# Moving state updates, one product and the weight sums between stages of a fused decoder layer

## The chip, the cores and the metric

The kernel runs on one core of a Trainium2 chip. A core has five engines that run side by side, each with its own queue of instructions: TensorE (PE in the profile, with PEld for its weight loads), VectorE (DVE), ScalarE (ACT), GpSimd (POOL) and SyncE (SP), which here issues nearly all DMA transfers. The metric is the device time of one execution in microseconds (us).

## The reference, cut to what matters

The layer works on x of shape (16, 256, 512), that is 4096 tokens of width 512, in fp32. It has three parts, each followed by a layer norm. The first is the one that the change touches, a state-space block:

```
xn   = x * rsqrt(mean(x*x) + EPS) * w_norm
proj = xn @ W_in.T                       # z (1024), xi (1024), dt (16), B (256), C (256)
xi   = silu(causal_conv4(xi))
dt   = softplus(dt + dt_bias);  dA = exp(dt * -exp(A_log))
u    = (dt * mean_over_head(xi))[..., None] * B
h_t  = dA_t * h_(t-1) + u_t ;  y_t = sum_n(h_t * C_t)      # a scan over 256 tokens
y    = (y @ W_h2i.T) * silu(z)
out  = y @ W_out.T + x
```

The second part is a long convolution with gating and the third a linear layer with a routed low-rank update; the change leaves both as they are.

## The kernel before, in words

**Groups.** The state-space block is worked in eight groups `g` of 512 tokens (two sequences of 256), in the loop of line 495. The second and third parts follow as 32 steps, from line 1062.

**Stages.** The large input product is split over ten pairs of output blocks. One pass over the list `order` (lines 561 and 562) is ten stages `i` = 0 to 9: x0, z0, x1, x2, z1, x3, then b0 (stage 6), c1 (stage 7), z2 (8), z3 (9). Each pair is multiplied by a Strassen-like scheme with seven half-size products in place of eight. The first four products (`first_products`) fill two PSUM banks `al` and `be`; `first_sums` reads those (one ScalarE copy, three VectorE adds, lines 319 to 322); `last_products` then adds the other three products on top, and `last_sums` reads these (one ScalarE operation, two VectorE adds, lines 332 to 334). So TensorE can't start the last products of a pair until VectorE has done that pair's first sums.

**Shift between the engines.** In stage `i` TensorE does the first products of pair `i` and then the last products of pair `i-1`. VectorE does the first sums of pair `i` and then the last sums of pair `i-1`; after an x pair it also does the convolution of two channel blocks (`mixed`, one scaling and six multiply-adds for the two, lines 524 to 528, partly on ScalarE).

**States.** In stages 6 and 8 `head_means` forms the head means on TensorE (line 538) for the two halves `ht` of the state rows. In stage 7 `states(0, ...)` and in stage 8 `states(1, ...)` run on VectorE. Each is `m = xm * dtS` (line 549), `B = B * m` (line 550) and two scans over 256 tokens (line 553). `outputs(ht)` multiplies the states by C (line 558). C is the output of pair 7, whose last sums VectorE does in stage 8 (`finish_sums`, line 618). In stage 9 TensorE sums the products over the state index into `yps` (line 596, two instructions for each half), in its queue behind the first products of pair 9 and in front of the last products of pair 8.

**Decays.** The generator `decays` (line 380) makes dt and dA on VectorE and ScalarE in small steps, writes them to DRAM (line 418) and issues three spreading loads (`spread`, line 430) into a pool of three buffers. The fourth, `spread(1, 1)`, is dA for the second half and reuses the buffer of the first, so SyncE holds it until `m` of the first half has been computed. For groups 1 to 7 these steps run in the output product of the previous group; in group 0 they run in stages 1, 2, 3, 5 and 6.

**Weight sums.** The Strassen scheme needs sums of weights. GpSimd forms those of the input weights (`weight_sums`, lines 213 to 216; those of z2 and z3 stand in the program in stages 6 and 7 of group 0), and of the output weights (`w_o_sums`, lines 270 to 278, in stage 8 of group 0). The output product of the group (`out_begin`, `out_middle`, line 685) uses `(0, 1)`, which holds the sum T3 in place, first, and then T1, T2 and T4.

**Order.** The order of the work on each engine is that of the program; no scheduler reorders it. Each engine takes its queue in order, and semaphores tie the engines.

Of the kernel before, what the change touches and what calls it, by code (L numbers as in the profile page):

```python
# [10 lines left out]
ALU = mybir.AluOpType  # L11
# [4 lines left out]
B, S, D = 16, 256, 512  # L16
# [49 lines left out]
def decoder_kernel(  # L66
# [24 lines left out]
    nc = tc.nc  # L91
# [73 lines left out]
    with ExitStack() as s1:  # L165
# [36 lines left out]
        A11, A12, A22, S3, S1, S2, S4 = range(7)  # L202
# [47 lines left out]
        HC = NI // 2  # L250
# [13 lines left out]
        parts = [q2.tile([P, 2, S], F32, tag="vT", name="w_o_sum") for _ in range(2)]  # L264
        parts += [q3.tile([P, 3, S], F32, tag="cT", name="w_o_sum") for _ in range(3)]
        parts = [t[:, k, :] for t in parts for k in range(t.shape[1])]
        for k, name in enumerate(("T1", "T2", "T4")):
            w_o[name] = parts[k * HC : (k + 1) * HC]

        def w_o_sums():  # L270

            sub = nc.gpsimd.tensor_tensor
            for c in range(HC):
                sub(w_o["T1"][c], w_o[0, 1][c], w_o[0, 0][c], ALU.subtract)
                sub(w_o[0, 1][c], w_o[1, 1][c], w_o[0, 1][c], ALU.subtract)
            for c in range(HC):
                sub(w_o["T2"][c], w_o[1, 1][c], w_o["T1"][c], ALU.subtract)
                sub(w_o["T4"][c], w_o[1, 0][c], w_o["T2"][c], ALU.subtract)
        xis = [p1.tile([P, GB, S + 3], F32, name=f"xi{i}") for i in range(4)]
        for t in xis:  # L280
            nc.gpsimd.memset(t[:, :, 0:3], 0.0)
# [35 lines left out]
        def first_sums(al, be, to):  # L317
            u = p2.tile([P, S], F32, tag="u", name="u", bufs=3)
            nc.scalar.copy(u, al[:, 0:S])
            nc.vector.tensor_tensor(u, u, al[:, S:], ALU.add)  # L320
            nc.vector.tensor_tensor(to[3], u, be[:, S:], ALU.add)
            nc.vector.tensor_tensor(to[3], to[3], be[:, 0:S], ALU.add)
            return u
# [56 lines left out]
        def decays():  # L380

            d_lg = ps_t.tile([P, 2, P], F32, tag="tr", name="d_lg")
            d, lg = d_lg[:, 0, :], d_lg[:, 1, :]
            for kc in range(KD):
                for q in range(TT):
                    nc.tensor.matmul(
                        d[32 * q : 32 * (q + 1), :],
                        w_dt[:, kc, :],  # L390
                        xnT[:, kc, q * P : (q + 1) * P],
                        start=(kc == 0),
                        stop=(kc == KD - 1),
                    )
            yield
            two = p1.tile([P, 2, P], F32, tag="two", name="two")
            e, u1 = [p1.tile([P, P], F32, tag=n, name=n) for n in ("e", "u1")]
            dt, dA = two[:, 0, :], two[:, 1, :]
            nc.vector.tensor_scalar_add(dt, d, dtb)
            nc.vector.scalar_tensor_tensor(e, dt, -1.0, dt, ALU.mult, ALU.max)  # L400
            nc.scalar.activation(e, e, AF.Exp, scale=-1.0)
            yield
            nc.vector.tensor_scalar_add(u1, e, 1.0)
            nc.scalar.activation(lg, u1, AF.Ln)
            yield
            same = dA
            nc.vector.tensor_scalar(same, u1, 1.0, None, ALU.is_equal)
            nc.vector.tensor_tensor(lg, lg, same, ALU.add)
            nc.vector.scalar_tensor_tensor(u1, u1, -1.0, same, ALU.add, ALU.add)
            nc.vector.reciprocal(u1, u1)  # L410
            nc.vector.tensor_tensor(lg, lg, u1, ALU.mult)
            nc.vector.tensor_tensor(lg, lg, e, ALU.mult)
            nc.vector.scalar_tensor_tensor(dt, dt, 0.0, lg, ALU.max, ALU.add)
            yield

            nc.scalar.activation(dA, dt, AF.Exp, scale=A)
            for q in range(TT):
                nc.sync.dma_start(
                    both[:, :, q * P : (q + 1) * P].rearrange("x h t -> h x t"),
                    two[32 * q : 32 * q + H1],  # L420
                )
            spreads[:] = [spread(*a) for a in ((0, 0), (1, 0), (0, 1))]
            yield
# [3 lines left out]
        def spread(x, ht):  # L427

            t = p2.tile([P, GT], F32, tag="spread", name="spread", bufs=3)
            nc.sync.dma_start(  # L430
                t,
                both[x, ht * HH : (ht + 1) * HH, :].unsqueeze(1).to_broadcast([HH, NST, GT]),
            )
            return t
# [60 lines left out]
        for g in range(NG):  # L495
# [48 lines left out]
                    )  # L544
                return xm

            def states(ht, xm, dtS, dAS):
                m = p2.tile([P, GT], F32, tag="acc", name="m", bufs=6)
                nc.vector.tensor_tensor(m, xm, dtS, ALU.mult)
                nc.vector.tensor_tensor(Bs[ht], Bs[ht], m, ALU.mult)  # L550
                for b in range(GB):
                    one = Bs[ht][:, b * S : (b + 1) * S]
                    nc.vector.tensor_tensor_scan(
                        one, dAS[:, b * S : (b + 1) * S], one, 0.0, ALU.mult, ALU.add
                    )
# [26 lines left out]
            for i, (kind, p) in enumerate(order):  # L582
# [21 lines left out]
                    finish_products()  # L604
                to = places(kind, p)
                u = first_sums(al, be, to)
                if g == 0:
                    if i == 1:
                        parts = decays()
                    if i in (1, 2, 3, 6):  # L610
                        next(parts)
                    if i == 6:
                        weight_sums(nc.gpsimd, w_z, 2)
# [7 lines left out]
                if g == 0 and i == 7:  # L621
                    weight_sums(nc.gpsimd, w_z, 3)
                if i == 7:
                    states(0, ms[0], *spreads[:2])
                    spreads.append(spread(1, 1))
                if i == 8:
                    outputs(0)
                    states(1, ms[1], *spreads[2:])
                    outputs(1)
                    if more:  # L630
                        rt = to_dram(rms(xs_next))
                    if g == 0:
                        w_o_sums()
                before = (kind, p, al, be, u, to)
                if i < 2 and late:
                    normalised(g - 1, late.pop(0))
# [46 lines left out]
            def out_product(ps, n, a, b, start=False, stop=False, upon=False):  # L683
                for c in range(HC):
                    nc.tensor.matmul(  # L685
                        ps,
                        own[a][c][:, n * P : (n + 1) * P],
                        w_o[b][c],
                        start=start and c == 0,
                        stop=stop and c == HC - 1,  # L690
                        skip_group_check=upon,
                    )

            def out_begin(n):

                al, be = [
                    bank() if n else ps_s.tile([P, 512], F32, tag="s", name="s")
                    for _ in range(2)
                ]
                out_product(al[:, 0:S], n, (0, 0), (0, 0), start=True)  # L700
                out_product(be[:, S:], n, "S3", (0, 1), start=True)
                return al, be

            def out_middle(n, al, be):
# [578 lines left out]
```

## Time and profile before

The time before is 1504.72 us, the median of three runs (1504.67 to 1504.87). The page describes one profiled execution.

| what | value |
|---|---|
| median of the runs | 1504.72 us |
| the profiled execution's own time | 1506.76 us |
| its span, first to last instruction | 1505.0 us |
| mean granted TensorE clock | 0.998 |
| TensorE busy | 1484.1 us, 99% |
| TensorE weight loads busy | 936.7 us, 62% |
| VectorE busy | 1184.4 us, 79% |
| ScalarE busy | 372.1 us, 25% |
| GpSimd busy | 363.3 us, 24% |
| HBM traffic over the span | 64 GB/s |

The page gives the busy time of each engine, the span in forty slices, the chain of work that ended last, and groups of instructions by line. The list of waits says, for each engine and line, how long the engine sat idle and which instruction ended that, with the total, the number of times and the longest, all in us. The timeline gives start and duration in us, engine, line, what is written and read, the shape, and how often the instruction is repeated; idle time before it stands in brackets. The first part takes the span up to about 770 us, one group being about 93 us.

### The profile page before, as it was taken

Reading aid. Unit: us, or ns where it says so; the run is one execution under the profiler, and the core shown is the slowest. Engines: PE = TensorE matmul, PEld = TensorE weight load, DVE = VectorE, ACT = ScalarE, POOL = GpSimd, SP = SyncE. Lnnn points to the kernel's source line nnn. Section 1 sums busy time; section 2 is a strip of 40 time slices with the busy share of each in tenths; the row PEclk is TensorE's granted clock in tenths of the full one; section 3 lists DMA queues with packets and bytes.
Section 4 is the critical chain, followed back from the end, with each engine's and each line's share of the span. In section 5 each row is a group of like instructions: output and inputs, shape, how many; then the busy total and the mean of one; then the engine's idle time right before and its main releaser. Section 6 shows DMA issues by size and latency. Waiting matters only on the chain.

```text
span 1505.0 us, 18707 instructions
## 1 busy us (share of the span) xinstructions
PE 1484.1 (99%) x6952; PEld 936.7 (62%) x6952; DVE 1184.4 (79%) x2132; ACT 372.1 (25%) x843; POOL 363.3 (24%) x528
## 2 busy tenths in 40 slices
PE   9999999999999999999999999999999999999997
PEld 8778788787887878878754444444444444444443
DVE  5978778787787877878667787788788778778776
ACT  2523223232232322323101122122122122122121
POOL 7140010100101001010012343343343243243242
PEclk9999999999999999999999999999999999999999
DMA  8014111121111211112022212212212212212200
GB/s 284 30 36 132 23 64 43 36 79 31 56 42 36 79 43 51 36 36 86 8 95 70 80 54 77 82 53 77 84 49 78 84 50 77 84 50 78 84 32 21
DMA packets 50810, 97.46 MB, mean 65 GB/s; under 512 B 10656, under 2 KB 15008, under 8 KB 50720
## 3 DMA queue, kind: packets, MB, share of 16 engines
q1 hardware_dynamic: 50192, 96.28, 20.1%
q8 instruction: 54, 0.88, 0.2%
q14 instruction: 36, 0.29, 0.1%
q10 hardware_dynamic: 528, 0.00, 0.0%
HBM read 78.95 MB, written 17.32 MB: 64 GB/s over the span
## 4 chain that ended last, share of the span: by engine, by line
PE 89%; DVE 3%; POOL 3%; issue 3%; DMA 1%; SPq 0%; POOLq 0%; ACT 0%; DVEq 0%; ACTq 0%
PE y L899 22%; PE mm L297 16%; PE y L913 12%; PE s L297 9%; PE base L1103 7%; PE s L685 6%; PE mm L685 5%; PE base L1059 2%; PE gl L1098 2%; PE tr L983 1%; PE mm L771 1%; PE mm L644 1%; PE xm L538 1%; PE tr L140 1%; DMA w_f<-in_WffnT 1%
## 5 line engine op out<-in xcount | busy, mean ns | idle before, releaser
L899 PE MATMUL y<-kv 128*128 128x512 f32 x768 | 348.4, 597 | 0.3 <-DVE pr L946 0.3
L946 DVE TENSOR_TENSOR pr<-y,cT 128x1024 f32<-128x1024 f32 x126 | 148.5, 1220 | 131.3 <-PE y L913 126.0
L899 PEld LDWEIGHTS y<-kv 128*128 128x128 f32 x768 | 141.4, 191 | 159.5 <-issue 155.4
L913 PE MATMUL y<-kv 64*64 64x512 f32 x1536 | 181.3, 602 | 3.1 <-DVE pr L946 1.6
L152 DVE TENSOR_TENSOR kv<-vT,cT 128x1024 f32<-128x1024 f32 x128 | 150.4, 1217 | 1.5 <-ACT vT L142 1.5
L528 DVE SCALAR_TENSOR_TENSOR acc<-xi,wc,acc 128x512 f32<-128x512 f32 x192 | 145.2, 770 | 5.7
L956 DVE TENSOR_REDUCE red<-pr 128x128 f32<-128x1024 f32 x126 | 147.1, 1209 | 0.0
L913 PEld LDWEIGHTS y<-kv 64*64 64x64 f32 x1536 | 52.5, 132 | 122.9 <-issue 97.0
L1103 PE MATMUL base<-w_f,ol 128*128 128x512 f32 x248 | 111.5, 592 | 0.0
L297 PE MATMUL mm<-XT,w_z 128*128 128x256 f32 x384 | 90.7, 379 | 0.0
L345 POOL TENSOR_TENSOR rstd<-ms,nhalf 128x4 f32<-128x4 f32 x8 | 8.1, 1018 | 294.5 <-DVE ms L343 294.5
L297 PEld LDWEIGHTS mm<-XT,w_z 128*128 128x128 f32 x384 | 73.0, 190 | 9.9
L61 POOL TENSOR_TENSOR rs_a<-ve_a,nhalf 128x1 f32<-128x1 f32 x32 | 19.0, 593 | 244.8 <-DVE ve_a L59 244.8
L827 POOL TENSOR_TENSOR sk<-kv,skip_bc 128x512 f32<-128x512 f32 x32 | 47.4, 1480 | 116.9 <-DVE kv L152 116.9
L1103 PEld LDWEIGHTS base<-w_f,ol 128*128 128x128 f32 x248 | 44.8, 190 | 44.5 <-issue 44.5
L297 PE MATMUL mm<-xnT,w_z 128*128 128x256 f32 x288 | 70.2, 380 | 1.2 <-DVE u L320 1.2
L969 POOL TENSOR_SCALAR nm_c<-sum_c 128x1 f32<-128x1 f32 x31 | 7.2, 232 | 249.4 <-DVE x L1023 249.4
L297 PEld LDWEIGHTS mm<-xnT,w_z 128*128 128x128 f32 x288 | 54.6, 190 | 12.6 <-issue 3.8
L297 PE MATMUL s<-XT,w_xi 128*128 128x256 f32 x256 | 60.5, 379 | 0.4 <-DVE XT L206 0.4
L297 PE MATMUL mm<-XT,w_xi 128*128 128x256 f32 x256 | 60.5, 379 | 0.0
L974 ACT ACTIVATE sq<-x,nm_c 128x512 f32<-128x512 f32 x31 | 22.4, 722 | 136.8 <-POOL nm_c L969 132.5
L297 PEld LDWEIGHTS s<-XT,w_xi 128*128 128x128 f32 x256 | 48.6, 190 | 7.3 <-POOL w_xi L216 0.8
(258 smaller groups left out, 2544.7 us busy)
## 6 DMA issues: line engine op xcount, KB each, us to landing
kv<-in_toep SPq DMA_DIRECT2D x32, 640.0 KB
cT<-in_ctxT SPq DMA_DIRECT2D x32, 384.0 KB
xt<-in_x SPq DMA_DIRECT2D x32, 256.0 KB
xnT<-in_xT SPq DMA_DIRECT2D x8, 1024.0 KB
spread<-both SPq DMA_DIRECT2D x32, 256.0 KB
first<-xt SPq DMA_DIRECT2D x32, 256.0 KB
vn<-first SPq DMA_DIRECT2D x32, 256.0 KB
out<-res SPq DMA_DIRECT2D x31, 256.0 KB
```

Source lines behind the costliest of these rows:

```text
L152: last = nc.vector.tensor_tensor(kv[:, q, k * BQ : (k + NL // 2) * BQ], vT[:, q, blks].rearrange("p k (b i) -> p (k b) i", i=NH).unsqueeze ...
L297: nc.tensor.matmul(ps, w[:, p, a, kc, :], Xs[b][:, kc, :], start=start and kc == 0, stop=stop and kc == 1, skip_group_check=upon,)
L528: nc.vector.scalar_tensor_tensor(acc, xi[:, :, k : k + S], wc[:, c, k : k + 1], acc, ALU.mult, ALU.add)
L685: nc.tensor.matmul(ps, own[a][c][:, n * P : (n + 1) * P], w_o[b][c], start=start and c == 0, stop=stop and c == HC - 1, skip_group_check=upon,
L827: nc.gpsimd.tensor_tensor(sk, own, skip_bc[:, h * NH : (h + 1) * NH].unsqueeze(1).to_broadcast(full), ALU.mult,)
L899: nc.tensor.matmul(bank_of(y, lb), T[:, PAIRS.index((lb, mb)), :], moving(kv, q, mb), start=not late and lb not in begun, stop=stop, skip_ ...
L913: return nc.tensor.matmul(bank_of(y, lb)[cols], T[rows, len(PAIRS) + lb, cols], moving(kv, q, lb)[rows], start=start, stop=False, skip_gro ...
L946: nc.vector.tensor_tensor(pr.rearrange("p (k b j) i -> p k b j i", k=2, j=NH), y[i].rearrange("p k (b j i) -> p k b j i", j=NH, i=NH), cT[ ...
L956: nc.vector.tensor_reduce(red[:, q, 2 * i : 2 * i + 2, :].rearrange("p k t -> p (k t)"), pr, AX.X, ALU.add)
L1059: nc.tensor.matmul(base, turned[0], w_lb, start=False, stop=True)
L1098: nc.tensor.matmul(gl, o_l[:, kc, :], w_gl[:, kc, :], start=(kc == 0), stop=(kc == KD - 1))
L1103: nc.tensor.matmul(base, o_l[:, kc, :], w_f[:, kc, :], start=(kc == 0), stop=False)
```

## The change

There are four edits. (1) The first multiplication of `states` becomes a function of its own, `stepped`. For the first half it moves from stage 7 to stage 6 in groups 1 to 7 (in front of the last sums of pair 5), and in group 0 to a place further ahead in stage 7 (in front of the last sums of pair 6); the load `spread(1, 1)` moves with it. (2) In stage 8 the whole of `states(1, ...)` moves from behind `outputs(0)` to a place in front of the last sums of pair 7. (3) In `decays` one product moves from VectorE to GpSimd, `e = u1 * e`, and the product ahead of it is written to SBUF instead of PSUM. (4) The sum T3 of the output weights gets its own tiles and is made first, ahead of the other work of GpSimd in stage 8; T1 takes the place of the weights that it is made from. The number of instructions on the large engines stays the same, apart from the one product that changes engine.

```diff
--- before.py
+++ after.py
@@ -264,18 +264,23 @@
         parts = [q2.tile([P, 2, S], F32, tag="vT", name="w_o_sum") for _ in range(2)]
         parts += [q3.tile([P, 3, S], F32, tag="cT", name="w_o_sum") for _ in range(3)]
         parts = [t[:, k, :] for t in parts for k in range(t.shape[1])]
-        for k, name in enumerate(("T1", "T2", "T4")):
+        for k, name in enumerate(("T3", "T2", "T4")):
             w_o[name] = parts[k * HC : (k + 1) * HC]
 
         def w_o_sums():
 
             sub = nc.gpsimd.tensor_tensor
+            w_o["T1"] = w_o[0, 1]
+            for c in range(HC):
+                sub(w_o["T3"][c], w_o[1, 1][c], w_o[0, 1][c], ALU.subtract)
+            yield
             for c in range(HC):
                 sub(w_o["T1"][c], w_o[0, 1][c], w_o[0, 0][c], ALU.subtract)
-                sub(w_o[0, 1][c], w_o[1, 1][c], w_o[0, 1][c], ALU.subtract)
             for c in range(HC):
                 sub(w_o["T2"][c], w_o[1, 1][c], w_o["T1"][c], ALU.subtract)
                 sub(w_o["T4"][c], w_o[1, 0][c], w_o["T2"][c], ALU.subtract)
+            yield
+
         xis = [p1.tile([P, GB, S + 3], F32, name=f"xi{i}") for i in range(4)]
         for t in xis:
             nc.gpsimd.memset(t[:, :, 0:3], 0.0)
@@ -408,9 +413,9 @@
             nc.vector.tensor_tensor(lg, lg, same, ALU.add)
             nc.vector.scalar_tensor_tensor(u1, u1, -1.0, same, ALU.add, ALU.add)
             nc.vector.reciprocal(u1, u1)
-            nc.vector.tensor_tensor(lg, lg, u1, ALU.mult)
-            nc.vector.tensor_tensor(lg, lg, e, ALU.mult)
-            nc.vector.scalar_tensor_tensor(dt, dt, 0.0, lg, ALU.max, ALU.add)
+            nc.vector.tensor_tensor(u1, lg, u1, ALU.mult)
+            nc.gpsimd.tensor_tensor(e, u1, e, ALU.mult)
+            nc.vector.scalar_tensor_tensor(dt, dt, 0.0, e, ALU.max, ALU.add)
             yield
 
             nc.scalar.activation(dA, dt, AF.Exp, scale=A)
@@ -544,9 +549,12 @@
                     )
                 return xm
 
-            def states(ht, xm, dtS, dAS):
+            def stepped(xm, dtS):
                 m = p2.tile([P, GT], F32, tag="acc", name="m", bufs=6)
                 nc.vector.tensor_tensor(m, xm, dtS, ALU.mult)
+                return m
+
+            def states(ht, m, dAS):
                 nc.vector.tensor_tensor(Bs[ht], Bs[ht], m, ALU.mult)
                 for b in range(GB):
                     one = Bs[ht][:, b * S : (b + 1) * S]
@@ -604,6 +612,14 @@
                     finish_products()
                 to = places(kind, p)
                 u = first_sums(al, be, to)
+                if i == 8:
+                    states(1, stepped(ms[1], spreads[2]), spreads[3])
+                if i == 6 and g:
+                    ms = [stepped(ms[0], spreads[0])]
+                    spreads.append(spread(1, 1))
+                if i == 7 and not g:
+                    ms = [stepped(ms[0], spreads[0])]
+                    spreads.append(spread(1, 1))
                 if g == 0:
                     if i == 1:
                         parts = decays()
@@ -621,16 +637,17 @@
                 if g == 0 and i == 7:
                     weight_sums(nc.gpsimd, w_z, 3)
                 if i == 7:
-                    states(0, ms[0], *spreads[:2])
-                    spreads.append(spread(1, 1))
+                    states(0, ms[0], spreads[1])
+                if g == 0 and i == 8:
+                    w_sums = w_o_sums()
+                    next(w_sums)
                 if i == 8:
                     outputs(0)
-                    states(1, ms[1], *spreads[2:])
                     outputs(1)
                     if more:
                         rt = to_dram(rms(xs_next))
                     if g == 0:
-                        w_o_sums()
+                        next(w_sums)
                 before = (kind, p, al, be, u, to)
                 if i < 2 and late:
                     normalised(g - 1, late.pop(0))
@@ -698,7 +715,7 @@
                     for _ in range(2)
                 ]
                 out_product(al[:, 0:S], n, (0, 0), (0, 0), start=True)
-                out_product(be[:, S:], n, "S3", (0, 1), start=True)
+                out_product(be[:, S:], n, "S3", "T3", start=True)
                 return al, be
 
             def out_middle(n, al, be):
```

## The prediction

> **What bounds the kernel.** The page first: one engine fills the span.
>
> ```profile
> PE 1484.1 (99%) x6952; PEld 936.7 (62%) x6952; DVE 1184.4 (79%) x2132; ACT 372.1 (25%) x843; POOL 363.3 (24%) x528
> ```
>
> The chain that ended last gives PE 89%. Only time in which PE stands still, 1505.0 - 1484.1 = 20.9 us, can be won here, since no edit removes a matmul. The list of waits of PE says where; of its twelve lines these three touch the edits:
>
> ```profile
> PE yps L596 <- DVE b L558: 4.5, 8, 1.0
> PE mm L297 <- DVE u L320: 1.2, 1, 1.2
> PE s L685 <- POOL w_o_sum L277: 0.9, 1, 0.9
> ```
>
> The first comes once a group, 1.0 in group 0 and 0.5 in the others. The timeline of group 2 from the end of stage 8, VectorE alone:
>
> ```profile
> 260.12 1.27 DVE L553 TENSOR_TENSOR_SCAN b<-spread,b 128x256 f32<-128x256 f32 x2
> 261.31 0.39 DVE L320 TENSOR_TENSOR u<-u,mm 128x256 f32<-128x256 f32 x1
> ...
> 264.25 0.42 DVE L333 TENSOR_TENSOR c<-u,mm 128x256 f32<-128x256 f32 x1 [1.56 <-PE mm L297]
> 264.58 0.41 DVE L334 TENSOR_TENSOR c<-u,mm 128x256 f32<-128x256 f32 x1
> 264.92 0.69 DVE L558 TENSOR_TENSOR b<-b,c 128x512 f32<-128x512 f32 x1
> 265.52 0.69 DVE L549 TENSOR_TENSOR m<-xm,spread 128x512 f32<-128x512 f32 x1
> 266.24 0.69 DVE L550 TENSOR_TENSOR b<-b,m 128x512 f32<-128x512 f32 x1
> 266.96 1.27 DVE L553 TENSOR_TENSOR_SCAN b<-spread,b 128x256 f32<-128x256 f32 x2
> 268.27 0.69 DVE L558 TENSOR_TENSOR b<-b,c 128x512 f32<-128x512 f32 x1
> ```
>
> and PE of the same stretch:
>
> ```profile
> 267.50 1.02 PE L596 MATMUL yps<-b,sel 128*128 128x512 f32 x2
> 269.02 1.13 PE L596 MATMUL yps<-b,sel 128*128 128x512 f32 x2 [0.50 <-DVE b L558]
> 269.98 0.59 PE L297 MATMUL mm<-xnT,w_z 128*128 128x256 f32 x2
> ```
>
> VectorE idles 1.56 us for C, then does the second half's states, which need no C; PE waits for their end. In group 0 VectorE is a stage behind and has no such hole. The timeline there, same six multiply-adds three times:
>
> ```profile
> 41.30 6.08 DVE L528 SCALAR_TENSOR_TENSOR acc<-xi,wc,acc 128x512 f32<-128x512 f32 x6
> 49.78 4.57 DVE L528 SCALAR_TENSOR_TENSOR acc<-xi,wc,acc 128x512 f32<-128x512 f32 x6
> 61.36 4.56 DVE L528 SCALAR_TENSOR_TENSOR acc<-xi,wc,acc 128x512 f32<-128x512 f32 x6
> ```
>
> The first has GpSimd's sums of z2 and z3 beside it (38.1 to 45.25), the others nothing.
>
> **What the Trainium skill says.** "SBUF — State Buffer", section "SBUF: two separate sides": VectorE with two SBUF inputs and GpSimd exclude each other for a whole instruction. The trace agrees: with GpSimd busy throughout (24.97) the six take 6.77, and a GpSimd sum 1.17 in place of 0.73; VectorE's sums with a PSUM input keep 0.42. "TensorE: Matmul & The Clock Gate", section "Architectural detail": VectorE and GpSimd are strict FIFO; so a waiting GpSimd product holds everything behind it. "GPSIMD Engine Reference", section "4.1 Engine selection": GpSimd can't touch PSUM, hence `u1` as its input.
>
> **Part 1, groups 1 to 7.** Removed: the first `m` (0.68) leaves stage 7. In stage 6 it falls between 249.25 (end of L322) and 250.97, where VectorE waits 1.72 us for PE: free, its inputs being long there (xm ended at 244.7, its load is of the previous group). Without that cover it would cost 0.7 of VectorE, against 4.3 us by which PE's next user (last products of pair 7 at 261.35, L320 done at 257.04) is later. Stage 7 ends 0.7 earlier; L320 of stage 8 can start at 260.7, L322 ends at about 261.95. Then `m` 0.72, `b` 0.72, scans 1.3 (steps from start to start): 264.7. PE has C's products ready at 264.2, so the C sums run without a wait: 0.67, outputs 0.60 + 0.70, done at 266.7 against 268.96. The `spread(1, 1)` moves past no other issue on SP (none stands between stages 1 and 8) and goes out at about 250; before it went at 259.31 and its traffic ended at 262.4, so it is never late.
>
> PE reaches `yps` at 267.50 and now needs no stop. Eight matmuls of 512 columns elsewhere (139.91 to 143.34) step by 0.429; four end at 267.50 + 1.715 = 269.215, and the next now starts at 269.98. Gain 0.765, more than the listed 0.50, because ends of matmuls are modelled and the first step after a stop is 0.1 longer. Seven groups: **-5.4 us**. What is late next? SP's row load moves up with VectorE; the next input load, the output product and the 32 steps hang on PE and shift with it. I find no second wait behind this one. Bounds: 7 x 0.50 = -3.5 to 7 x 0.80 = -5.6; I take -5.4.
>
> **Part 2, GpSimd product, groups 1 to 7.** No row shows it. GpSimd's 128x512 difference takes 1.27 and its 128x256 0.73, so 128x128 about 0.46; with signals of 0.08 and 0.04 (112.12 to 112.20, 227.01 to 227.04), VectorE's next starts 0.58 after L411 instead of 0.36: +0.22. Bounds: 0 to +0.7 (a GpSimd operation on 4 columns takes 1.02). Behind it on VectorE stand the norm statistics and the next first sums (L320 done at 214.45, PE needs it at 216.76): 2.3 us of cover, 0 us paid. Only in group 1 does PE stop on that chain (131.05, 0.3 us after the even step): **+0.2**.
>
> **Part 3, group 0.** The product stands in stage 5, ahead of z2's and z3's sums in GpSimd's queue. These ran at 38.1; now they wait for L411, about 56.4. So:
> - The multiply-adds at 41.30 and the scaling ahead of them run alone: from 40.35 to the next L320 5.00 instead of 6.94, -1.94. PE's stop at 47.76 (even step 46.36; with a slow start 1.6 lost) goes.
> - The multiply-adds of stage 6 start at 60.84 - 1.94 + 0.22 = 59.1. GpSimd has z2's sums until 60.3 (PE needs them at 62.9), z3's with 1.16 each until 65, then T3's. So 7.23 (24.43 to 31.66) instead of 5.00: end at 66.35, 0.5 later than 65.84.
> - PE's second head means (67.39) need the silu of that result, 0.8 later: 67.15. PE waits there from 65.8. Of the 1.6 won, 0.25 is left.
> - From here VectorE runs without a hole as before, 10.67 to the end of outputs(1): 77.0 instead of 76.5. Both halves of `yps` now wait: the second starts at 77.25 instead of 76.57: **+0.7**. The fourth spread load lands about 3 us after issue (its traffic ran from 69.8 to 71.4 after an issue near 68.5); the scan needs it at 73.8.
> - T3 is done by 68.5. But I don't believe that the 0.9 at 88.02 is T3's: L275 ended at 83.70, while VectorE's L334, which reads the `be` bank to be overwritten, ended at 87.93, delayed by sums at 83.77 that took 3.49 for 1.43 beside GpSimd. T1, T2 and T4 still run there, to 87.5: **-0.15**. If it is T3's, -1.1.
>
> **Sum.** -5.4 + 0.2 + 0.7 - 0.15 = -4.65 us. The profiled span of 1505.0 becomes 1500.35; what lies around it (1506.76 - 1505.0 = 1.76) stays, and this execution is 2.04 above the median. The difference carried to the median: 1504.72 - 4.65 = **1500.1**.
>
> **Rivals.**
> - Group 0 gains too. If the exclusion in stage 6 costs less than 7.23 (sums and multiply-adds interleave), up to -1.6 at 47.76, -1.3 at `yps` and -1.1 at 88.02 are kept: 1496.5 to 1499.0. For it: the list books two of these on work that moves. Against: at 24.97 full exclusion was measured. 15%.
> - The gain is half. The wait at `yps` is worth its listed 0.50, or group 0 loses 2 to 3 through the head means: 1501.5 to 1504.0. For it: group 0 has no hole for anything added. 17%.
> - Slower: GpSimd's product holds VectorE in each group. Place: between L411 and L413. It decides when it costs over 2.3 us a group, the cover of PE's last products of pair 0; above that each 0.43 costs 7 x 0.43 = 3.0, and part 1's gain must be spent first (0.77), so from about 3.5 us: 1508. Against: the dearest GpSimd operation of such size took 1.4. 4%.
> - The edits do nothing: the program order does not set VectorE's order, or PE's wait comes from elsewhere; 1504.7. Against: VectorE's timeline follows the program everywhere. 4%.
>
> **How the numbers follow.** The main case, 1499.0 to 1501.5, has 60%. No change means within 0.2%, 3.0 us, about what a measurement of this kernel can tell. Main case and the first rival are faster, and a fifth of the second: 0.78. The rest of it and the last: 0.17; slower 0.05. The range 1498.2 to 1502.6 leaves out the far end of the first rival, half of the second and the last two.
>
> **What would show it.** Right: no `yps` wait in groups 1 to 7, VectorE's hole before the C sums gone, `m` of the first half in the hole of stage 6; in group 0 z2's sums after 56, no stop at 47.76, a new stop at the second head means, a longer one at `yps`. Wrong: a `yps` wait left in later groups, PE idle in stages 7 or 8, or group 0 ending more than 2 us later than before.

## The result, and the profile after

The changed kernel takes 1501.61 us, the median of 13 runs (1500.02 to 1504.75), against 1504.82 us of the kernel before in the same comparison (13 runs, 1504.66 to 1506.56). The ratio is 0.9976, with a 95% interval of 0.9967 to 0.9984: 3.2 us are gained. The forecast was 1500.1 us, in a range of 1498.2 to 1502.6.

The busy line of the page of the changed kernel:

```profile
PE 1480.3 (99%) x6952; PEld 936.5 (62%) x6952; DVE 1179.8 (79%) x2124; ACT 372.1 (25%) x843; POOL 367.9 (25%) x536
```

TensorE still fills the span, 1499.8 us. The eight products that left VectorE stand on GpSimd (2132 to 2124 instructions, and 528 to 536). TensorE idles 19.5 us in place of 20.9. Its busy time fell as well, by 3.8 us with the same number of matmuls: 1.7 of that is a matter of the clock (below), and 7 x 0.26 = 1.8 comes from the modelled ends at `yps`, where 1.02 + 1.13 of two parts became 1.88 of one. So the list of waits alone would have understated what a stop is worth.

The list of waits of TensorE in the changed kernel (engine, tile and line, what ended the wait, then us in total, times, longest):

```profile
PE yps L604 <- DVE b L566: 1.8, 1, 1.8
...
PE mm L302 <- DVE u L325: 1.2, 1, 1.2
...
PE xm L543 <- ACT acc L582: 0.9, 1, 0.9
PE s L702 <- DVE zs L339: 0.5, 1, 0.5
```

The wait at `yps`, which came eight times, comes once, in group 0, and is longer there. A wait at the second head means is new. The line of 1.2 us has the same text as before, but it is another stop: the one at 47.76 is gone, and this one lies in group 1. The wait at the output product is now listed against VectorE's last sums, no longer against GpSimd's sums.

Group 2 of the changed kernel, timeline of VectorE, from stage 6 to stage 8:

```profile
250.39 0.68 DVE L554 TENSOR_TENSOR m<-xm,spread 128x512 f32<-128x512 f32 x1
252.19 0.42 DVE L338 TENSOR_TENSOR xi<-u,mm 128x256 f32<-128x256 f32 x1 [1.11 <-PE mm L302]
...
263.02 0.68 DVE L554 TENSOR_TENSOR m<-xm,spread 128x512 f32<-128x512 f32 x1
263.74 0.69 DVE L558 TENSOR_TENSOR b<-b,m 128x512 f32<-128x512 f32 x1
264.46 1.27 DVE L561 TENSOR_TENSOR_SCAN b<-spread,b 128x256 f32<-128x256 f32 x2
265.66 0.40 DVE L338 TENSOR_TENSOR c<-u,mm 128x256 f32<-128x256 f32 x1
265.97 0.41 DVE L339 TENSOR_TENSOR c<-u,mm 128x256 f32<-128x256 f32 x1
266.30 1.28 DVE L566 TENSOR_TENSOR b<-b,c 128x512 f32<-128x512 f32 x2
```

TensorE in the same stretch:

```profile
268.72 1.88 PE L604 MATMUL yps<-b,sel 128*128 128x512 f32 x4
270.43 1.89 PE L302 MATMUL mm<-xnT,w_z 128*128 128x256 f32 x8
```

The first `m` stands in VectorE's hole of stage 6, of which 1.11 us are left. The second half's states fill the hole of 1.56 us ahead of the C sums, so the outputs are done at 267.6, more than a microsecond before TensorE reaches `yps`, and its four matmuls run without a stop.

Where the time went is read off TensorE's own starts, changed kernel minus kernel before:

| place | before | after | difference | new since the line above |
|---|---|---|---|---|
| pair 4, group 0, the even step ahead of the old stop | 46.36 | 46.61 | +0.25 | +0.25 (start of the program) |
| first matmul behind `yps`, group 0 | 77.53 | 78.84 | +1.31 | +1.06 |
| output product of group 0 (S3 by T3) | 88.02 | 88.91 | +0.89 | -0.42 |
| stop in group 1 | 131.05 | 133.03 | +1.98 | +1.09 |
| behind `yps`, group 1 | 176.76 | 177.98 | +1.22 | -0.76 |
| behind `yps`, group 2 | 269.98 | 270.43 | +0.45 | -0.77 |
| behind `yps`, group 7 | 736.07 | 732.71 | -3.36 | -3.81 (five groups) |

At the end of the state-space block the changed kernel is 3.36 us ahead, close to the gain of the medians. The two profiled spans differ by more, 5.2 us, and most of the rest lies where the two programs do the same. TensorE at the start of the second part, the kernel before and then the changed one:

```profile
774.55 4.50 PE L913 MATMUL y<-kv 64*64 64x512 f32 x24 [1.51 <-DVE xt L786]
```

```profile
771.14 2.81 PE L930 MATMUL y<-kv 64*64 64x512 f32 x24 [1.74 <-DVE xt L803]
```

The same 24 matmuls took 4.50 us in one execution and 2.81 in the other. The granted clock was 0.77 between 772 and 778 us in the first, 1.00 in the second. More on this at the end.

The lines that answer to the three runs of six multiply-adds in group 0, with the GpSimd product between them, timeline of VectorE in the changed kernel:

```profile
41.15 4.56 DVE L533 SCALAR_TENSOR_TENSOR acc<-xi,wc,acc 128x512 f32<-128x512 f32 x6
...
48.13 4.56 DVE L533 SCALAR_TENSOR_TENSOR acc<-xi,wc,acc 128x512 f32<-128x512 f32 x6
...
56.34 0.29 DVE L416 TENSOR_TENSOR u<-d_lg,u 128x128 f32<-128x128 f32 x1
57.27 0.80 DVE L418 SCALAR_TENSOR_TENSOR two<-two,e 128x128 f32<-128x128 f32 x1 [0.64 <-POOL e L417]
57.99 0.41 DVE L325 TENSOR_TENSOR u<-u,s 128x256 f32<-128x256 f32 x1
...
60.48 6.78 DVE L533 SCALAR_TENSOR_TENSOR acc<-xi,wc,acc 128x512 f32<-128x512 f32 x6
```

and GpSimd there:

```profile
56.78 0.46 POOL L417 TENSOR_TENSOR e<-u,e 128x128 f32<-128x128 f32 x1 [18.40 <-DVE u L416]
57.20 0.73 POOL L213 TENSOR_TENSOR w_z<-w_z 128x256 f32<-128x256 f32 x1
```

The contention has moved from the first run (6.08 before) to the third (4.56 before). GpSimd's product takes 0.46 us. But 0.42 us after its start the first of the held-up weight sums starts, just ahead of VectorE's next small step, which takes 0.80 instead of 0.29.

TensorE in group 0 pays for it twice, at the head means and at `yps`:

```profile
67.97 1.04 PE L543 MATMUL xm<-acc,mean 128*32 128x512 f32 x2 [0.88 <-ACT acc L582]
...
77.05 1.95 PE L604 MATMUL yps<-b,sel 128*128 128x512 f32 x4 [1.79 <-DVE b L566]
```

The stop in group 1, timeline of TensorE and then of VectorE:

```profile
133.03 1.13 PE L302 MATMUL mm<-xnT,w_xi 128*128 128x256 f32 x4 [1.24 <-DVE u L325]
```

```profile
131.62 0.49 DVE L478 TENSOR_TENSOR w_f<-w_f,ident 128x128 f32<-128x128 f32 x2 [1.24 <-DMA w_f<-in_WffnT]
...
132.57 0.41 DVE L325 TENSOR_TENSOR u<-u,mm 128x256 f32<-128x256 f32 x1
```

VectorE adds the identity to the weights of the third part, `w_f`, ahead of the first sums that TensorE needs. It waits 1.24 us for the load of `w_f`. The same step in the kernel before:

```profile
129.63 0.50 DVE L473 TENSOR_TENSOR w_f<-w_f,ident 128x128 f32<-128x128 f32 x2 [0.21 <-DMA w_f<-in_WffnT]
```

### The profile page after: what moved, and what is told of

It reads as the page before. It is cut to its first block, busy times and chain, and to the rows that moved or that the text cites. A ratio compares the mean times of both kernels' runs of the same rounds, so it can differ in the third digit from the quotient of the medians.

```text
span 1499.8 us, 18739 instructions
## 1 busy us (share of the span) xinstructions
PE 1480.3 (99%) x6952; PEld 936.5 (62%) x6952; DVE 1179.8 (79%) x2124; ACT 372.1 (25%) x843; POOL 367.9 (25%) x536
## 4 chain that ended last, share of the span: by engine, by line
PE 92%; DVE 5%; DMA 1%; issue 1%; ACT 0%; POOL 0%; SPq 0%; POOLq 0%; DVEq 0%
PE y L916 22%; PE mm L302 17%; PE y L930 12%; PE s L302 11%; PE base L1120 7%; PE s L702 6%; PE mm L702 5%; PE base L1076 2%; PE gl L1115 2%; DVE acc L533 1%; PE tr L1000 1%; PE mm L788 1%; PE mm L661 1%; PE yps L604 1%; PE xm L543 1%; PE tr L140 1%
```

## The experiments

**The states' reorder alone.** The kernel before with the first two edits of the change.

```diff
...
+                if i == 8:
+                    states(1, stepped(ms[1], spreads[2]), spreads[3])
+                if i == 6 and g:
+                    ms = [stepped(ms[0], spreads[0])]
+                    spreads.append(spread(1, 1))
+                if i == 7 and not g:
+                    ms = [stepped(ms[0], spreads[0])]
+                    spreads.append(spread(1, 1))
...
-                    states(0, ms[0], *spreads[:2])
-                    spreads.append(spread(1, 1))
+                    states(0, ms[0], spreads[1])
...
-                    states(1, ms[1], *spreads[2:])
```

> The kernel before with the reordered states alone (first multiplication in stage 6 or further ahead in stage 7, second half's states ahead of the last sums of pair 7), the product of the decays on VectorE and the weight sums of GpSimd as before. Theory: the seven later groups give their 7 x 0.765 = 5.35 us, group 0 is nearly unchanged (same VectorE work without a hole; both halves of yps now wait, +0.2), so 5.0 to 5.3 us faster than before, faster than the whole change; the yps wait is left in group 0 alone and TensorE's stop of 1.2 at stage 5 of group 0 stays. Rival (the reorder itself costs group 0 the 1 us that the changed kernel loses there): 4.0 to 4.4 us faster.

Measured: 1499.23 us (five runs, 1499.19 to 1501.31; ratio 0.9964, 0.9951 to 0.9978), 5.6 us less than before and 2.4 less than the whole change. One line of its waits answers to the eight:

```profile
PE yps L599 <- DVE b L561: 1.0, 1, 1.0
```

The whole gain of the change is in this part. With the other two added, 2.4 us of it are lost.

**The GpSimd product alone.** The kernel before with the third edit.

```diff
-            nc.vector.tensor_tensor(lg, lg, u1, ALU.mult)
-            nc.vector.tensor_tensor(lg, lg, e, ALU.mult)
-            nc.vector.scalar_tensor_tensor(dt, dt, 0.0, lg, ALU.max, ALU.add)
+            nc.vector.tensor_tensor(u1, lg, u1, ALU.mult)
+            nc.gpsimd.tensor_tensor(e, u1, e, ALU.mult)
+            nc.vector.scalar_tensor_tensor(dt, dt, 0.0, e, ALU.max, ALU.add)
```

> The kernel before with the product of the decays on GpSimd alone. Theory: the product holds back the sums of z2 and z3 in GpSimd's queue until about 57 us, where they slow the multiply-adds of stage 6 instead of those of stage 4. TensorE's stop at stage 5 of group 0 (1.6 us) goes, but VectorE ends stage 8 at about the same time or up to 0.8 later, so the gain is given back at yps: 0 to 0.8 us slower than before. Rival (the stop removed is a gain that stays): 1.2 to 1.6 us faster.

Measured: 1505.33 us (13 runs; ratio 1.0005, 0.9997 to 1.0013), 0.5 more, not to be told from nothing. The stop at 47.76 is gone here too. The timeline of VectorE in group 0 shows what is paid for it:

```profile
56.81 0.80 DVE L413 SCALAR_TENSOR_TENSOR two<-two,e 128x128 f32<-128x128 f32 x1 [0.64 <-POOL e L412]
...
60.02 6.08 DVE L528 SCALAR_TENSOR_TENSOR acc<-xi,wc,acc 128x512 f32<-128x512 f32 x6
```

So the 1.6 us that the product wins at 47.76 are lost again, at the head means (a wait of 0.2) and at `yps` (longest wait there 1.8 in place of 1.0): behind `yps` TensorE starts at 77.71, before at 77.53. In group 1 the product alone brings no stop; VectorE doesn't wait for `w_f` there.

**T3's tiles and order alone.** The kernel before with the fourth edit.

```diff
-        for k, name in enumerate(("T1", "T2", "T4")):
+        for k, name in enumerate(("T3", "T2", "T4")):
...
+            w_o["T1"] = w_o[0, 1]
+            for c in range(HC):
+                sub(w_o["T3"][c], w_o[1, 1][c], w_o[0, 1][c], ALU.subtract)
+            yield
...
+                if g == 0 and i == 8:
+                    w_sums = w_o_sums()
+                    next(w_sums)
```

> The kernel before with the sum T3 in tiles of its own and first in GpSimd's queue of stage 8, nothing else. Theory: GpSimd has no work before it, so T3 runs at 45 to 49 us right behind the sums of z3, beside the multiply-adds of VectorE: the stop of TensorE at stage 5 of group 0 grows from 1.2 to about 2, yps in group 0 waits 0.7 longer, and the wait of 0.9 at the first output product stays or shrinks by 0.4, since it is VectorE's last sums that end it: 0.3 to 0.8 us slower than before. Rival (that wait is for T3): 0.6 to 1.1 us faster.

Measured: 1506.95 us (21 runs, 1505.22 to 1508.99; ratio 1.0011, 1.0005 to 1.0018). It is slower, by more than expected. Two places show it. Without the product in front, nothing holds GpSimd back, and T3's four sums run on behind z3's at 45.3, beside the first run of multiply-adds. (By the count of stages used here that run belongs to stage 3, though expectations of other runs call it that of stage 4; TensorE's stop behind it, at 47.76 in the kernel before, is in stage 5.) VectorE in group 0, and TensorE in group 1:

```profile
41.42 6.76 DVE L533 SCALAR_TENSOR_TENSOR acc<-xi,wc,acc 128x512 f32<-128x512 f32 x6
```

```profile
132.60 1.68 PE L302 MATMUL mm<-xnT,w_xi 128*128 128x256 f32 x6 [1.08 <-DVE u L325]
```

The stop in stage 5 of group 0 grows from 1.2 to 1.9 us, and the stop of group 1 is there, with a wait of 1.15 us for `w_f`. T3 itself is done by 49.5, and the wait at the output product is still 0.7 us, listed against VectorE's last sums: that wait wasn't T3's.

The three parts alone make -5.6 + 0.5 + 2.1 = -3.0 us; the change made -3.2.

**The changed kernel with earlier constants.** Six loads, `w_f` among them, are issued in stage 1 of group 0 instead of behind the first output product.

```diff
                 if i == 1 and more:
                     xs_next = load_x(g + 1)
+                if i == 1 and g == 0:
+                    skip_bc = wp.tile([P, S], F32, name="skip_bc")
+                    nc.sync.dma_start(skip_bc, skip.partition_broadcast(P))
...
+                    w_f = wp.tile([P, KD, D], F32, name="w_f")
+                    nc.sync.dma_start(w_f, WffnT.rearrange("(k p) o -> p k o", p=P))
...
             if g == 0:
-                skip_bc = wp.tile([P, S], F32, name="skip_bc")
...
```

> The changed kernel with the six loads of constants for the later parts (w_f among them) issued in stage 1 of group 0 instead of behind group 0. Theory: w_f came late in the changed kernel (VectorE waited 1.24 us for it at 131.6, and TensorE 1.24 us for VectorE), because SyncE held the loads behind the writing and spreading of the decays: 1.0 to 1.6 us faster than the changed kernel, 4.3 to 5.0 us faster than before, and a narrower spread of times. Rival (the wait at 131.6 is VectorE's own lateness): within 0.4 us of the changed kernel.

Measured: 1500.25 us (five runs, 1500.05 to 1501.73; ratio to the kernel before 0.9968, 0.9955 to 0.9980), 1.4 less than the changed kernel. The two intervals overlap, but four of the five runs lie at 1500.05 to 1500.26, where the changed kernel has two of 13. TensorE in group 1, with no idle time in brackets:

```profile
131.37 2.11 PE L302 MATMUL mm<-xnT,w_xi 128*128 128x256 f32 x8
```

The stop in group 1 is the load's. Of the 1.5 us by which the change falls short of the forecast, it is the largest part (0.9, below).

**The changed kernel with the product back on VectorE.** The third edit undone, the rest of the change kept.

```diff
-            nc.vector.tensor_tensor(u1, lg, u1, ALU.mult)
-            nc.gpsimd.tensor_tensor(e, u1, e, ALU.mult)
-            nc.vector.scalar_tensor_tensor(dt, dt, 0.0, e, ALU.max, ALU.add)
+            nc.vector.tensor_tensor(lg, lg, u1, ALU.mult)
+            nc.vector.tensor_tensor(lg, lg, e, ALU.mult)
+            nc.vector.scalar_tensor_tensor(dt, dt, 0.0, lg, ALU.max, ALU.add)
```

> The changed kernel with the one product of the decays back on VectorE; the states' order and the own tiles of T3 stay. Theory A (the three parts add up, each with the price that it showed alone: -5.6 for the states, +0.5 for the product, about +2 for T3): 1504.8 - 5.6 + 2 = 1501.2 us, range 1500.6 to 1501.8, no measurable gain over the changed kernel. TensorE's stop of 1.2 at about 47.7 is back, its waits at the second head means and most of the longer one at yps are gone, and the stop of group 1 on the late weights of the next part stays. Theory B (the product's place in front of GpSimd's next sum is what costs group 0 its 1.05 us, and the stop taken away at 47.7 is not worth what it seemed): 1500.0 to 1500.5, the longer wait at yps gone and no stop in its place that costs more than 0.5.

Measured: 1501.69 us (21 runs, 1499.70 to 1505.65; ratio 0.9975, 0.9969 to 0.9982), the time of the change. Theory A holds: the wait at `yps` goes from 1.8 to 1.0, the one at the head means disappears, and a stop of 1.9 us is back in stage 5 of group 0. Within the change the product moves a wait, and no gain of it can be measured. The stop of group 1 stays without the product, and VectorE waits 1.25 us for `w_f` there. TensorE:

```profile
132.42 2.11 PE L302 MATMUL mm<-xnT,w_xi 128*128 128x256 f32 x8 [1.18 <-DVE u L325]
```

**The reorder alone with earlier constants.** The first experiment's edit and the fourth's together.

```diff
+                if i == 1 and g == 0:
+                    skip_bc = wp.tile([P, S], F32, name="skip_bc")
...
-                    states(1, ms[1], *spreads[2:])
```

> The kernel before with the states' reorder and, beside it, the six loads of constants for the next parts issued in stage 1 of group 0 in place of group 1. Theory A (the late load costs only where the spread's issue in the first output product comes late, which was seen only together with the T3 tiles): nothing to gain here, 1499.2 us as with the reorder alone, within 0.4. Theory B (early constants are worth 1.4 us by themselves): about 1497.9 us.

Measured: 1499.16 us (five runs, 1499.01 to 1500.93; ratio 0.9964, 0.9950 to 0.9977), the 1499.23 of the reorder alone. Early constants brought something only where T3's part was in.

**Weight sums held to a better place.** The one before, and GpSimd's sums of z2 and z3 wait for the first sums of stage 5. An addition of one column, overwritten at once by the sum behind it, makes them wait.

```diff
+        def hold(t, first):
+            nc.gpsimd.tensor_tensor(first[:, 0:1], t[:, 0:1], t[:, 0:1], ALU.add)
...
-                    if i == 6:
+                    if i == 5:
+                        hold(u, w_z[:, 2, S1, 0])
                         weight_sums(nc.gpsimd, w_z, 2)
+                        weight_sums(nc.gpsimd, w_z, 3)
...
-                if g == 0 and i == 7:
-                    weight_sums(nc.gpsimd, w_z, 3)
```

> As the kernel before it in this list (states' reorder and early constants), and in group 0 GpSimd's weight sums of z2 and z3 are held back by an addition of one column that reads the first sums of stage 5; the product of the decays stays on VectorE. Theory A (what cost time in group 0 was the place of these sums: beside the multiply-adds of stage 4 as before, or beside those of stage 6 as in the change; between the two VectorE reads PSUM for most of the time and they are cheap): the stop at 47.7 goes (1.2 listed, 1.6 lost), the multiply-adds of stages 4 and 6 both take 4.56 us; some of it comes back where the small steps of the decays in stage 5 meet the sums. 1497.4 to 1498.6 us. Theory B (VectorE has no hole in group 0, so whatever it is delayed by in stage 5 comes back in full at yps): 1498.9 to 1499.5 us, the stop at 47.7 gone and a longer one at yps.

Measured: 1497.61 us (five runs, 1497.49 to 1499.30; ratio 0.9953, 0.9940 to 0.9965). This is 7.1 us less than the kernel before, 4 less than the change, and 1.55 less than the same kernel without the hold (four of the five runs lie below all five of that kernel). Timeline of VectorE in group 0, and GpSimd's:

```profile
40.79 4.56 DVE L531 SCALAR_TENSOR_TENSOR acc<-xi,wc,acc 128x512 f32<-128x512 f32 x6
...
54.86 0.52 DVE L412 SCALAR_TENSOR_TENSOR u<-u,two 128x128 f32<-128x128 f32 x1
...
59.76 4.56 DVE L531 SCALAR_TENSOR_TENSOR acc<-xi,wc,acc 128x512 f32<-128x512 f32 x6
```

```profile
52.73 0.20 POOL L271 TENSOR_TENSOR w_z<-u 128x1 f32<-128x1 f32 x1 [14.71 <-DVE u L323]
53.00 0.73 POOL L213 TENSOR_TENSOR w_z<-w_z 128x256 f32<-128x256 f32 x1
...
58.10 0.72 POOL L216 TENSOR_TENSOR w_z<-w_z 128x256 f32<-128x256 f32 x1
```

Theory A holds. The eight sums fit between 53.0 and 58.8, where VectorE mostly reads PSUM. All three runs of multiply-adds take 4.56, GpSimd's sums stay at 0.73 to 0.78, and VectorE's small steps in between lose about 0.2 us each in two places (L412 took 0.52 for 0.28). The stop in stage 5 is gone and the wait at `yps` stays at 1.1.

**The same with T3's part, in held steps.** T3 in stage 7, T1 in stage 8, T2 and T4 at the end.

```diff
+                    if i == 7:
+                        hold(u, w_o["T3"][0])
+                        w_sums = w_o_sums()
+                        next(w_sums)
+                    if i == 8:
+                        hold(u, w_o["T2"][0])
+                        next(w_sums)
```

> As the one before it in this list, and T3 gets its own tiles and is made in stage 7 of group 0, T1 in stage 8, T2 and T4 at the end, each step held by an addition of one column. Theory A (the sums of the output weights delay the output product through VectorE's last sums at 87.9, and spread out over stages 7 to 9 they delay less): 0.3 to 0.8 us less than the one before it, the wait at the output product below 0.2 us. Theory B (as with the T3 tiles alone: more sums beside VectorE's steps that read SBUF in stages 7 and 8, where group 0 has no slack): 0.3 to 1.0 us more, with the wait at yps longer by that.

Measured: 1501.66 us (six runs, two at 1498.3 and four from 1501.56 to 1502.91; ratio 0.9972, 0.9961 to 0.9984). The profiled execution is one at 1498.3. Its wait at the output product is gone, as theory A said, but VectorE in stages 7 and 8 shows theory B:

```profile
66.87 1.02 DVE L562 TENSOR_TENSOR b<-b,m 128x512 f32<-128x512 f32 x1
...
71.53 1.27 DVE L562 TENSOR_TENSOR b<-b,m 128x512 f32<-128x512 f32 x1
72.84 1.68 DVE L565 TENSOR_TENSOR_SCAN b<-spread,b 128x256 f32<-128x256 f32 x2
```

The states' steps, 0.69 and 1.27 when alone, are drawn out by the sums beside them, and TensorE's wait at `yps` is 2.9 us in place of 1.1. Why four of the six runs lie 3.4 us above the other two the one profile, of a low run, can't show.

**What makes the load of `w_f` late.** The loads stand on SyncE's queue behind the spreading loads, and those wait until the rows of the decays have landed in DRAM (the list of SyncE's waits names the writes of the rows). In the profiles, between the end of the last row's issue and the first spread's issue of group 1 stood 1.2 us in every kernel without T3's part, and 2.4 to 3.2 us in every one with it. Two kernels split this part: one has the tiles of the change and the old place of the sums, the other the old tiles and an early place (T1 is made first).

Tiles only:

```diff
+        for k, name in enumerate(("T3", "T2", "T4")):
...
+            w_o["T1"] = w_o[0, 1]
...
+                sub(w_o["T3"][c], w_o[1, 1][c], w_o[0, 1][c], ALU.subtract)
```

Early sums only:

```diff
                 sub(w_o["T1"][c], w_o[0, 1][c], w_o[0, 0][c], ALU.subtract)
+            yield
+            for c in range(HC):
                 sub(w_o[0, 1][c], w_o[1, 1][c], w_o[0, 1][c], ALU.subtract)
...
+                if g == 0 and i == 8:
+                    w_sums = w_o_sums()
+                    next(w_sums)
```

> The kernel before with T3 in tiles of its own and T1 in the place of its source, but all sums of the output weights left where they were (stage 8, behind the input norm). In every kernel with the T3 part the spread's issue in the first output product came 2.4 to 3.2 us after the last issue of the rows in DRAM, in every kernel without it 1.2 us. Theory A (it comes with GpSimd's work being done earlier): 1.2 us here, the stop of group 1 stays near 0.3 us or nothing, 1504.8 us within 0.5. Theory B (it comes with the tiles, that is with what lies where): 2.4 to 3.2 us here too, a stop of about 1.1 us in group 1, about 1505.9 us.

> The kernel before with T1 (in its own tiles, as before) made first in stage 8, where the change makes T3; T3 is still formed in place, later. The tiles are those of before, GpSimd's order is that of the change. Theory A (the late spread comes with GpSimd's earlier work): 2.4 to 3.2 us between the issues, a stop of about 1.1 us in group 1, and beside it the 0.7 us that four more sums next to the multiply-adds of stage 4 cost: 1506.5 us. Theory B (it comes with the tiles): 1.2 us, no stop in group 1, and only the 0.7: 1505.5 us.

Measured: tiles only 1505.19 us (12 runs, 1504.68 to 1507.95; ratio 1.0003, 0.9995 to 1.0012), early sums only 1507.24 us (12 runs, 1504.98 to 1507.97; ratio 1.0009, 1.0000 to 1.0018). Neither time decides: early sums only is slower than either theory said, and its profiled execution (1507.80 us) has two drops of TensorE's clock, of which the last section shows one. SyncE's queue decides, tiles only and then early sums only:

```profile
112.00 1.73 SPq L419 DMA_DIRECT2D both<-two  x4
116.72 1.83 SPq L431 DMA_DIRECT2D spread<-both  x3
```

```profile
113.08 1.73 SPq L422 DMA_DIRECT2D both<-two  x4
115.98 1.84 SPq L434 DMA_DIRECT2D spread<-both  x3
```

Tiles only: 116.72 - 113.73 = 2.99 us, and TensorE stops in group 1:

```profile
132.86 1.46 PE L298 MATMUL mm<-xnT,w_xi 128*128 128x256 f32 x5 [1.52 <-DVE u L321]
```

Early sums only: 115.98 - 114.81 = 1.17 us, and no stop there. So in these profiles the late landing comes with the tiles, not with the time at which GpSimd works: theory B. Over all twelve profiled executions the split holds, six with the tiles and six without. What in the tiles makes the landing late stays open. The median of the tiles alone rose by only 0.6 us, and the profiled execution is one of the five slower ones of twelve (1506.25 and above; the other seven end at 1505.24 or below). So the late landing need not occur in every execution; only profiled ones show it.

## Why the prediction was right, and what was mis-sized

All the signs named for a right forecast came. Of those named for a wrong one, only TensorE's idle time in stage 8 is there, in group 0 alone, and it is the stop at the second head means that was itself forecast. What follows goes through the terms.

**Part 1 was right in mechanism and size.** -0.765 a group was forecast, and -0.76 and -0.77 stand in groups 1 and 2. The choice of 0.765 over the listed 0.50 was the right one: four matmuls of 512 columns without a stop lead to a next start 0.77 earlier. Seven groups make 5.34 against 5.4, and the reorder alone gave 5.6. The cover holds too: `m` in the hole of stage 6, C sums without a wait, no second wait behind.

**Part 2, groups 1 to 7: the price was right, and nothing is paid.** From L416 to L418 it is 0.92 us in place of 0.66, +0.26 against a forecast of +0.22.

**The term "only in group 1, +0.2" was mis-sized: +1.09.** TensorE stops there on VectorE, as the forecast says, but the step named the product as what lengthens that chain, and it is the load of `w_f`: the product alone brings no stop, the stop stays when the product is taken back, and it goes when the loads are issued early. The sign that the load was on this chain stood in the trace before (VectorE waited 0.21 us for it), and the forecast gave T3's own tiles, with which the load comes late, no cost at all. This one term is 0.9 of the 1.5 us by which the forecast is off.

**Part 3, group 0: the path was right, +1.06 in place of +0.7.** The stop at 47.76 went, the multiply-adds of stage 6 took 7.22 (59.96 to 67.18) where 7.23 was forecast, the head means became a stop, and `yps` a longer one. The failed step is "the multiply-adds of stage 6 start at 60.84 - 1.94 + 0.22". In group 0 the product cost 0.78, not 0.22: from L416 to the next L325 1.65 us (56.34 to 57.99), before it 0.87. GpSimd's next sum stood ready behind the product, and VectorE's L418 ran into it. The exclusion had been applied to the multiply-adds and not to the small step that waits for the product itself. So of the stop that went, nothing was left behind the head means, where the forecast kept 0.25: TensorE starts there at 68.94, before at 68.39. VectorE got a third of a microsecond back up to the outputs, 10.32 us (67.18 to 77.50) where 10.67 was forecast. That this total came near is in part luck: 0.56 was missing for the product, and 0.35 came back on VectorE unforeseen. About 0.15 of the difference between +1.06 and +0.7 stays open.

One reading behind this term is too strong. At 24.97 the forecast saw "full exclusion", an engine shut out for a whole instruction of the other. Alone, a multiply-add starts every 0.75 us and a GpSimd sum every 0.69; taking strict turns, a pair would need 1.44. Beside each other GpSimd's sums start about every 1.13 us there (25.48, 26.62, 27.75), so some 0.3 us of each pair still overlap. The 7.23 came true because it was read off this stretch, not worked out from the rule.

**The output product: right that the wait isn't T3's.** With T3 done early, 0.5 us of wait is left, listed against the last sums of VectorE. The shift is -0.42 against -0.15: the sums of `z_sum` beside GpSimd took 3.02 instead of 3.49, with GpSimd's last sum done at 87.8 where it was 90.2 before.

**What the sum left out.** +0.25 at the start of the program, taken for a spread between executions: in the ten kernels of the experiments the same place lies between 0.19 ahead of the kernel before and 0.12 behind it. The terms as measured: 0.25 + 1.06 - 0.42 + 1.09 - 5.34 = -3.36, against -4.65.

**The rivals.** 1501.61 us lies just outside the main case (1499.0 to 1501.5) and just inside "The gain is half" (1501.5 to 1504.0), though neither of that rival's two reasons is what happened; `yps` was worth its full 0.765 and group 0 lost 1, not 2 to 3. "Group 0 gains too" was wrong for the order of the change. It is right for another place of the same sums: held to stage 5, they give 1.55 us. "Slower through GpSimd's product" fell: it costs 0.26 us a group in cover of 2.3. "The edits do nothing" fell with the seven waits at `yps`.

## What to carry to other kernels

An engine that waits for late input while later work has its own input at hand should do the later work first: three moved blocks of code gave all of the 5.6 us here. Moving one product from VectorE to GpSimd brought nothing that could be measured, while moving GpSimd's sums to a time when VectorE mostly reads PSUM gave 1.55 us. The work that stands queued behind a new GpSimd instruction must be priced with it. A wait of 0.2 us on a load, on a chain that already stops the bounding engine, is a term of the forecast with a size of its own.

## What the hardware showed that was not expected

**A stop of under 2 us was followed, in some executions, by half of TensorE's clock.** In the kernel with early sums TensorE stops for 1.91 us in stage 5 of group 0. Its timeline behind the stop:

```profile
48.38 3.06 PE L301 MATMUL mm<-xnT,w_z 128*128 128x256 f32 x8 [1.91 <-DVE u L324]
51.23 1.76 PE L301 MATMUL mm<-XT,w_z 128*128 128x256 f32 x4
```

The same stretch in windows of 3 us (window, length, busy time and count of PE, PEld, DVE, ACT and POOL, then TensorE's clock, DMA share, GB/s):

```profile
48.00:51.00 3.00, 2.62 (x8) 2.05 (x9) 2.82 (x7) 1.62 (x4) 1.26 (x2) 0.72 0.00 0
51.00:54.00 3.00, 3.00 (x15) 1.39 (x13) 2.89 (x5) 0.91 (x2) 0.00 (x0) 0.71 0.00 0
54.00:57.00 3.00, 3.00 (x14) 2.67 (x15) 2.83 (x8) 0.99 (x3) 0.00 (x0) 1.00 0.00 0
```

Windows of half a microsecond put it more finely: 0.50 in all six from 49.5 to 52.5, and 0.80 and 0.79 in the one ahead and the one behind. That makes 3.4 us at half speed, a loss of 1.7 us.

With the product back on VectorE, a stop of 1.92 us at the same place was followed by no drop: those eight matmuls took 2.11 us and the four 1.03, at a clock of 1.00. The profiled execution with early sums had a second drop at the start of the second part. So such a stop costs, in some executions, another 1.7 us (3.06 + 1.76 - 2.11 - 1.03). The Trainium skill, page "TensorE: Matmul & The Clock Gate", section "Part 1: The HAM clock gate", has an idle array at half speed, decided in windows of about 3.4 us that run freely. The trace agrees on the half and on the length. The page puts the drop after an idle window of that length; here the drop came after 1.9 us of standing still, and the measurement decides. That it depends on where the stop falls in a window, so that one such stop is followed by a drop and the next isn't, would fit, but no run here shows it. TensorE's stop at the start of the second part (1.5 us in the kernel before, 1.7 in the changed one) was followed by the same loss of 1.7 us in the profiled executions of the kernel before, of the changed kernel with earlier constants, of the one with the product back and of the one with early sums, and not in the other eight. That the spread of about 1.7 us between runs of one kernel, and the two levels of the kernel with T3 in held steps, have the same cause is only argued, and it can't be the whole of it: the profiled execution of tiles only lies 2 us above that kernel's fastest runs without such a drop. A stop that is taken away may thus be worth more than its length.

**VectorE's steps and GpSimd's sums drew each other out when they ran side by side.** A VectorE step of 0.29 us took 0.80, one of 0.69 took 1.27, and six multiply-adds took 6.78 for 4.56, while GpSimd's sums took up to 1.18 for 0.73. VectorE's adds with a PSUM input kept their 0.41 to 0.42 us.
